# Layer 2 of a four-layer graph network: tiles in stages one apart, TensorE's order fixed, own rows in the chunk buffer, a bank copied by ScalarE

## The chip, the core and the metric

One Trainium2 chip, of which the kernel uses one core. The metric is the device time of one execution in microseconds. A core has five engines that run side by side, each with its own queue of instructions, worked off in order: TensorE (PE in the profile; its weight loads are PEld), VectorE (DVE), ScalarE (ACT), GpSimd (POOL) and SyncE (SP), which here issues most of the DMAs. PE writes its sums into banks (PSUM), which DVE and ACT copy out. An engine waits for another by a semaphore at the head of an instruction; all that stands behind it on its queue waits with it.

## The reference

N = 2708 nodes, D = 512 features, a sparse adjacency matrix with an own entry for every node. Four layers, each with a normalisation ahead of it and a residual. Layers 0 and 1 (a normalised sum over an incidence matrix, and attention) are not touched. Layers 2 and 3 are:

```python
# layer 2
h = jnp.maximum(_layernorm(x, axis=-1), 0.0)
h2 = jax.nn.relu(adj @ (h @ W1) + b1)
h2 = jax.nn.relu(adj @ (h2 @ W3) + b3)
x = x + jnp.tanh(h2 @ Wf + bf)
# layer 3
h = jnp.maximum(_layernorm(x, axis=-1), 0.0)
A = (adj != 0)
x = x + A @ (h @ W + b) / jnp.sum(A, axis=0)[:, None]
```

## The kernel before

The nodes are cut into 22 row tiles of 128 (the last, number 21, called `NFULL`, has 20 rows). The sparsity of the matrix is used: for row tile m, the first `WHOLE[m]` column tiles (6 for the first tiles, then 4 or 3, 0 for tile 21) are multiplied densely; of the other columns only the listed ones are used, 128 to a chunk, `CHUNKS[m]` chunks (0 for tile 0, which takes all columns; 10 for tile 1, falling to 5, 2 for tile 21; 130 in all). For a chunk, POOL gathers 128 rows of the right-hand side from memory by an indirect DMA (L1032) into one of eight buffers `gg`, and PE multiplies them by the listed columns `ac`. The row tiles from 6 to 20 ("alone") don't have their own diagonal among either; their own rows are added by VectorE: a load of the tile's 128 rows (L1109), times the diagonal, plus the bias (L1110).

To keep single precision, dense products are made of three parts: high by high and low by low into a bank `main` (named `agg` in the aggregate), a shifted product into a bank `mixed` (`aggs`), and the result is main x (1 - EPS12) + mixed x EPS12. Listed chunks go into the second bank in full fp32 (L1086).

Layer 2 is three stretches:

- The first product (x W1) for all tiles, interleaved with the aggregate of tile 0.
- Pass 1 (L1185 to L1194), for each tile: `aggregated` (the aggregate A·g1, bias; then its transposes and the relu, `relu_parts`), `project3` with W3, sum of the banks into `go`, store to `g2d`. In pass 1 ACT also writes marks of the non-zeros (`nz`), which layer 3 uses.
- Pass 2 (L1378 to L1423), tiles in the order 0, 3 to 20 with 21 among them, 1, 2: `aggregated` over `g2d`, `project3` with Wf, bias, tanh (z), residual into x3, normalisation back into z, `relu_parts` of z, `project3` with W, bias, store to `hid` (and, for tiles from 3 on, to `hidr`). Layer 3 gathers rows of `hidr` and `hid` and multiplies them by the marks (L1283).

`aggregated` is: for each dense piece of up to three column tiles, a load of `raw` (L1015), ACT's high part a_hi (L1070), DVE's a_lo (L1071) and a_s (L1072), nine matmuls (L1083); then the chunks (L1086); then u is made from the two banks by two DVE operations (L1117). `relu_parts` is four PE transposes of u into a bank `pt` (L972), ACT's v_hi (L977), DVE's v_lo (L978) and v_s (L981). `project3` is twelve matmuls (L997): four with v_hi and four with v_lo into `main`, four with v_s into `mixed`. Of `main` and `mixed` there is one bank each; `agg`, `aggs` and `pt` have two each.

Buffers come from pools: `wp` gives two buffers to each name, among them u, which both the aggregate's sum (and the own row that is loaded into it) and z of pass 2 use, `go`, and the three v parts. `ap` gives two to `ac` and to the a parts, three to `raw` and `nz`.

The order of the instructions on an engine isn't the text's. The program is written tile by tile, one tile after the other; a scheduler at build time puts each engine's instructions in an order of its own, within what the data and the buffers allow. In pass 2 it puts, on PE, the four transposes of one tile's z next to the four of the next tile's u, one or two matmuls of a chunk behind them, and then both projections. A SP queue holds all loads and stores in one order: `ac`, `raw`, own rows, residual rows, stores of `hid` and `hidr`.

The lines that matter most:

```python
        if alone(m):
            nc.sync.dma_start(out=u, in_=gd[span(m)])            # L1109
            nc.vector.scalar_tensor_tensor(
                u, u, diag_c[:, m : m + 1], bias, op0=ALU.mult, op1=ALU.add
            )                                                     # L1110
            bias = u
        main, mixed = aggregate(m, parts, shifted, gd, marked)
```

Of the kernel before, what the change touches and what calls it, by code (L numbers as in the profile page):

```python
# [22 lines left out]
P = 128  # L23
# [21 lines left out]
def kernel(  # L45
# [36 lines left out]
    NB = (N + BLK - 1) // BLK  # L82
    UNIT = 4
    assert N % UNIT == 0
    NCH = 8 * ((max(CHUNKS) + 7) // 8)
    NCA = max(CHUNKS)
    NCL = max(CHUNKS[LEAD:])
# [63 lines left out]
    flag = const.tile([P, 1], I32, name="flag")  # L151


    idx_g = const.tile([P, NT, NCH], U32, name="idx_g")

    rdeg = const.tile([P, NT], FP, name="rdeg")
    diag_c, self_w = (const.tile([P, NT], FP, name=name) for name in ("diag_c", "self_w"))
# [81 lines left out]
    with tc.tile_pool(name="l0_slab", bufs=2) as slabs, tc.tile_pool(  # L239
# [177 lines left out]
        def search(m):  # L417

            first = dense_of(m) * P
            num = N - first  # L420
            ranks = ranks_of.pop(m)

            end = wp.tile([P, 1], FP, name="end")
            nc.vector.tensor_scalar_add(end, ranks[:, num - 1 : num], 1.0)
            nc.vector.tensor_copy(ranks[:, num : num + 1], end)
            want = wp.tile([P, NCH], FP, name="want")
            nc.vector.tensor_scalar(want, places, end, None, op0=ALU.min)
            for c0 in range(0, CHUNKS[m], 8):
                c = slice(c0, c0 + 8)
                at = wp.tile([P, 8], U32, name="found")  # L430
                nc.vector.max_index(at, want[:, c], ranks)
                nc.vector.tensor_scalar(
                    idx_g[:, m, c],
                    at,
                    float(N - first),
                    float(first),
                    op0=ALU.min,
                    op1=ALU.add,
                )
                node = wp.tile([P, 8], FP, name="node")  # L440
                nc.vector.tensor_scalar(
                    node,
                    at,
                    float(N - 1 - first),
                    float(N // UNIT),
                    op0=ALU.min,
                    op1=ALU.mult,
                )
                nc.vector.tensor_scalar_add(
                    idx_a[:, m, c], node, float((first * N + m * P) // UNIT)  # L450
                )
            nc.vector.tensor_scalar(
                bad[:, BAD_MANY + m : BAD_MANY + m + 1],
                end,
                float(CHUNKS[m] * P + 1),
                None,
                op0=ALU.is_gt,
            )
# [189 lines left out]
        def gather_rows(m):  # L648

            gs = []  # L650
            for c in range(CHUNKS[m]):
                g = hp.tile([P, D], FP, name=f"h{DENSE + gather_slot[0] % NGG}")
                gather_slot[0] += 1
                nc.gpsimd.indirect_dma_start(  # L654
                    out=g,
                    out_offset=None,
                    in_=h0d[:, :],
                    in_offset=bass.IndirectOffsetOnAxis(ap=idx_g[:, m, c : c + 1], axis=0),
                )
                gs.append(g)  # L660
            gathers[m] = gathers[m], gs
# [282 lines left out]
    order_2 = order_m[:1] + order_m[HEAD:] + order_m[1:HEAD]  # L944
    x3_last = dram.tile([P, D], FP, name="x3_last")

    idx_h = gp.tile([P, NT, NCA], U32, name="idx_h")
    NMARK = DENSE + NCA
    gather_slot = [0]

# [12 lines left out]
    def sum_banks_scaled(dst, main, mixed, n):  # L963

        nc.scalar.activation(dst[:n], main[:n], AF.Copy, scale=SHIFT - 1.0)
        nc.vector.tensor_tensor(dst[:n], mixed[:n], dst[:n], ALU.add)

    def relu_parts(v, n):

        pt = ps_t.tile([P, NCD, P], FP, name="pt")  # L970
        for c in range(NCD):
            nc.tensor.transpose(pt[:, c, :n], v[:n, c * P : (c + 1) * P], ident[:n, :n])  # L972
        hi, lo, s = (
            wp.tile([P, NCD, P], FR, name=f"v_{part}") for part in ("hi", "lo", "s")
        )
# [10 lines left out]
    def project3(parts, n, w, pool=None, names=("main", "mixed")):  # L986

        hi, lo, s = parts
        whi, wlo, ws = w
        main, mixed = ((pool or ps_p).tile([P, D], FP, name=name) for name in names)  # L990
        for acc, a, b, first, last in (
            (main, hi, whi, True, False),
            (main, lo, wlo, False, True),
            (mixed, s, ws, True, True),
        ):
            for c in range(NCD):
                nc.tensor.matmul(  # L997
                    acc[:n],
                    a[:, c, :n],
                    b[:, c, :],  # L1000
                    start=first and c == 0,
                    stop=last and c == NCD - 1,
                )
        return main, mixed

# [15 lines left out]
        return raw[:k, : len(ts), :n], k  # L1021

    def load_listed(m):
        ac = ap.tile([P, NCA, P], FP, name="ac")[:, : CHUNKS[m], : rows(m)]
        nc.sync.dma_start(out=ac, in_=listed[m])
        return ac

    def gather(m, gd, gs=None, index=idx_g):

        gs = gs or [gathered() for _ in range(CHUNKS[m])]  # L1030
        for c in range(CHUNKS[m]):
# [1 line left out]
                out=gs[c],  # L1033
                out_offset=None,
                in_=gd[:, :],
                in_offset=bass.IndirectOffsetOnAxis(ap=index[:, m, c : c + 1], axis=0),
            )
        return gs

    def aggregate(m, parts, shifted, gd, marked):  # L1040


        n = rows(m)
# [8 lines left out]
        mixed = ps_a.tile([P, D], FP, name="aggs")  # L1052
        chunks = []
        if num:
            ac = load_listed(m)
            chunks = [(ac[:, c, :], g) for c, g in enumerate(gather(m, gd))]
            if marked:
                mark(whole, ac)
        for ts in ([t for t in ts if t < whole] for ts in dense):
# [15 lines left out]
            for i, t in enumerate(ts):  # L1075
                ghi, glo, gs_ = gs[i]
                first, last = t == 0, t == whole - 1
                for acc, a, b, st, sp in (
# [1 line left out]
                    (main, lo, glo, False, last),  # L1080
                    (mixed, s, gs_, first, False),
                ):
                    nc.tensor.matmul(acc[:n], a[:k, i, :n], b[:k], start=st, stop=sp)  # L1083
        if chunks:
            for c, (a, g) in enumerate(chunks):
                nc.tensor.matmul(  # L1086
                    mixed[:n],
                    a,
                    g,
                    start=(c == 0 and not dense_of(m)),  # L1090
                    stop=(c == len(chunks) - 1),
                )
        else:
            for ts in others:
                gs = [shifted(t) for t in ts]
                raw, k = load_piece(m, ts)
                for i, t in enumerate(ts):
                    nc.tensor.matmul(  # L1098
                        mixed[:n], raw[:, i, :], gs[i][:k], start=False, stop=(t == NT - 1)
                    )  # L1100
        if marked:
            nc.sync.dma_start(out=nonzero[m], in_=nz[:, : whole + num, :n])
        return main, mixed

    def aggregated(m, parts, shifted, gd, bias, marked=False):
        n = rows(m)
        u = wp.tile([P, D], FP, name="u")
        if alone(m):
            nc.sync.dma_start(out=u, in_=gd[span(m)])  # L1109
            nc.vector.scalar_tensor_tensor(  # L1110
                u, u, diag_c[:, m : m + 1], bias, op0=ALU.mult, op1=ALU.add
            )
            bias = u
        main, mixed = aggregate(m, parts, shifted, gd, marked)
        if dense_of(m):
            for bank, scale in ((main, 1.0 - EPS12), (mixed, EPS12)):
                nc.vector.scalar_tensor_tensor(  # L1117
                    u[:n], bank[:n], scale, bias[:n], op0=ALU.mult, op1=ALU.add
                )
                bias = u  # L1120
        else:
            nc.vector.scalar_tensor_tensor(
                u[:n], mixed[:n], EPS12, bias[:n], op0=ALU.mult, op1=ALU.add
            )
        return relu_parts(u, n)

    def g_parts(t):
        return [gp.tile([P, D], FR, name=f"g{part}{t}") for part in ("hi", "lo", "s")]
# [53 lines left out]
    w3 = split_w(wsetb, wr, "wb")  # L1182
    wr = load_w(wset, wf_d, "wr")

    for m in order_m:  # L1185
        n = rows(m)
        parts = aggregated(m, first_parts, first_product, g1d, bias1, marked=True)
        if m == 0:
            wf = split_w(wset, wr, "wa")
            wr = load_w(wset, w_d, "wr")  # L1190
        main, mixed = project3(parts, n, w3)
        go = wp.tile([P, D], FP, name="go")
        sum_banks_scaled(go, main, mixed, n)
        nc.sync.dma_start(out=g2d[span(m)], in_=go[:n])  # L1194

    bf = load_bias(bf_d, "bias0")
    bl = load_bias(b_d, "bias2")
# [66 lines left out]
    def gather_h(m):  # L1264
# [1 line left out]
        whole, num = dense_of(m), CHUNKS[m]  # L1266
        nz = marks[m] = ap.tile([P, NMARK, P], U8, name="nz", bufs=3)
        nc.sync.dma_start(out=nz[:, : whole + num, : rows(m)], in_=nonzero[m])
        gd, index = (hidr, idx_h) if whole else (hid, idx_g)
        listed_h[m] = gather(m, gd, [next(places_h) for _ in range(num)], index)  # L1270

    def bank_h(m):
        if m not in banks:
# [30 lines left out]
    def listed_products(m):  # L1304
        n = rows(m)
        whole, num = dense_of(m), CHUNKS[m]
        mask = ap.tile([P, NCA, P], FR, name="ac")[:, :num, :n]
        nc.scalar.copy(mask, marks[m][:, whole : whole + num, :n])
        for c, g in enumerate(listed_h.pop(m)):
            high = part_room()  # L1310
# [64 lines left out]
    FIRST = 2  # L1375
    EARLY, FINAL = [list(range(HEAD, DENSE)), list(range(HEAD - 1))], [[HEAD - 1]]
    assert order_2[-1] == HEAD - 1
    for m in order_2:  # L1378
        n = rows(m)
        parts = aggregated(m, second_parts, second_product, g2d, bias3)  # L1380
        if m == 0:
            w = split_w(wsetb, wr, "wb")
        if dense_of(m) and m not in FULL:
            nc.vector.tensor_scalar_add(
                idx_h[:, m, : CHUNKS[m]], idx_g[:, m, : CHUNKS[m]], float(-HEAD * P)
            )
        if m == order_2[-1]:
            for k in order_3[:FIRST]:
                gather_h(k)
        main, mixed = project3(parts, n, wf)  # L1390
        z = wp.tile([P, D], FP, name="u")
        sum_banks(z, main, mixed, n)
        nc.vector.tensor_add(z[:n], z[:n], bf[:n])
        nc.scalar.activation(z[:n], z[:n], AF.Tanh)
        if m == NFULL:
            xt = wp.tile([P, D], FP, name="u")
        else:

            place = {order_2[-1]: "gs0", NSLOT: f"slot{order_2[-1]}"}.get(m, f"slot{m}")
# [3 lines left out]
        if m == NFULL:  # L1403
            nc.sync.dma_start(out=x3_last[:n], in_=xt[:n])
        norm(wp, xt, n, z)
        main, mixed = project3(relu_parts(z, n), n, w)
        go = wp.tile([P, D], FP, name="go")
        sum_banks(go, main, mixed, n)
        nc.vector.tensor_add(go[:n], go[:n], bl[:n])
# [9 lines left out]
            halves[m] = hi, lo  # L1419
        if alone(m):  # L1420
            nc.vector.scalar_tensor_tensor(
                xt, go, self_w[:, m : m + 1], xt, op0=ALU.mult, op1=ALU.add
            )  # L1423

# [460 lines left out]
```

## Time and profile before

Three runs: median 1456.13 us (1448.63 to 1460.58). The profiled execution took 1455.42 us, its span from the first to the last instruction is 1453.6 us, at a mean granted PE clock of 0.927.

| stretch of the span, us | what runs there | PE busy, us | granted clock | DMA share |
|---|---|---|---|---|
| 0 to 625 | layers 0 and 1, first product, tile 0 of pass 1 | | | |
| 625 to 905 | pass 1, tiles 1 to 21 | 258.17 | 0.95 | 0.77 |
| 905 to 1267.4 | pass 2, to the end of its last aggregate | 328.06 | 0.96 | 0.60 |
| 1267.4 to 1341 | last projections, start of layer 3 | 50.69 | 0.81 | 0.69 |
| 1341 to 1454 | rest of layer 3 | 98.71 | 0.95 | 0.77 |

Busy times of the other engines in pass 1: DVE 120.33, ACT 75.26, POOL 132.08 us; in 922 to 1245, the middle of pass 2 (323 us): DVE 202.79, ACT 136.89, POOL 118.84 us.

Durations of one instruction that the text below uses: an indirect gather about 1.02 us; DVE over 128x512 0.68 to 0.69 us, 0.75 with the diagonal (L1110); ACT's v_hi and its copy of a bank (L958) 0.60 us; a table load on ACT 1.28 us, two per tile in pass 2 (tanh and root); eight matmuls into `main` 1.85 us, four into `mixed` 0.92 us, a chunk of two records 0.86 us and eight transposes 0.87 us on the chain.

How to read the views: "A <- B: total, times, longest" is time in which an engine stood before A until B was done. In a timeline a line has start, duration, engine, line of the code, output and inputs, and in brackets the idle time before it and who ended it. The chain is the run of work that ended last, followed back from the end. A row of windows has the length, then busy time (and number of instructions) by engine, PE's granted clock (1.00 is full speed), the share of the DMA engines and GB/s. A matmul's duration is drawn with its end, so that matmuls one after the other overlap.

### The profile page before, as it was taken

Reading aid. Unit: us, or ns where it says so; the run is one execution under the profiler, and the core shown is the slowest. Engines: PE = TensorE matmul, PEld = TensorE weight load, DVE = VectorE, ACT = ScalarE, POOL = GpSimd, SP = SyncE. Lnnn points to the kernel's source line nnn. Section 1 sums busy time; section 2 is a strip of 40 time slices with the busy share of each in tenths; the row PEclk is TensorE's granted clock in tenths of the full one; section 3 lists DMA queues with packets and bytes.
Section 4 is the critical chain, followed back from the end, with each engine's and each line's share of the span. In section 5 each row is a group of like instructions: output and inputs, shape, how many; then the busy total and the mean of one; then the engine's idle time right before and its main releaser. Section 6 shows DMA issues by size and latency. Waiting matters only on the chain. (4 is left out here: it accounts for less than half of the span.)

```text
span 1453.6 us, 15184 instructions
## 1 busy us (share of the span) xinstructions
PE 1239.6 (85%) x4223; PEld 726.9 (50%) x4223; DVE 954.4 (66%) x2043; ACT 675.0 (46%) x1056; POOL 660.7 (45%) x674
## 2 busy tenths in 40 slices
PE   4888879888778569989998989899988888966997
PEld 2333334334333156655554556466645555555675
DVE  4686998788998478643443356356666656556776
ACT  5875467376344455432312224244444434435563
POOL 1245467666653431055463532334533232265773
PEclk9979999899889779999999989999999999978998
DMA  9989989899794497377776876756746555568995
GB/s 350 341 271 279 304 298 299 304 309 336 220 340 164 152 310 259 103 240 245 253 246 218 265 247 214 259 190 212 215 146 192 155 152 166 167 185 299 275 304 165
DMA packets 187750, 350.68 MB, mean 241 GB/s; under 512 B 22818, under 2 KB 96496, under 8 KB 183925
## 3 DMA queue, kind: packets, MB, share of 16 engines
q1 hardware_dynamic: 140057, 202.48, 41.8%
q0 software_dynamic: 46032, 145.05, 31.3%
q10 hardware_dynamic: 1568, 2.10, 0.4%
q8 instruction: 35, 0.57, 0.2%
q14 instruction: 58, 0.48, 0.1%
HBM read 285.96 MB, written 63.58 MB: 240 GB/s over the span
## 5 line engine op out<-in xcount | busy, mean ns | idle before, releaser
L1032 POOL DMA_INDIRECT gg<-g2d,idx_g x130 | 133.0, 1023 | 242.3 <-PE aggs L1086 199.1
L1086 PE MATMUL aggs<-gg,ac 128*128 128x512 f32 (+1 forms) x520 | 235.8, 595 | 4.7 <-DMA gg<-g1d,idx_g 4.7
L1032 POOL DMA_INDIRECT gg<-g1d,idx_g x130 | 132.3, 1018 | 174.1 <-PE aggs L1086 104.1
L864 PE MATMUL acc<-h,inc 128*128 128x512 f32 (+1 forms) x276 | 149.0, 687 | 47.3 <-DVE inc L704 43.6
L636 POOL DMA_INDIRECT ac<-in_adj_t_dram,idx_a x130 | 129.9, 999 | 101.4 <-issue 32.6
L1086 PEld LDWEIGHTS aggs<-gg,ac 128*128 128x128 f32 (+1 forms) x520 | 97.4, 190 | 104.7 <-issue 93.4
L654 POOL DMA_INDIRECT h<-h0d,idx_g x111 | 112.1, 1010 | 61.5 <-PE acc L864 33.8
L864 PEld LDWEIGHTS acc<-h,inc 128*128 128x128 f32 (+1 forms) x276 | 56.3, 217 | 113.2 <-issue 57.9
L977 ACT ACTIVATE v_hi<-pt 128x512 fp32r<-128x512 f32 (+1 forms) x88 | 48.6, 578 | 132.3 <-PE pt L972 126.3
L1083 PE MATMUL agg<-ghi,a_hi 128*128 128x512 f32 x180 | 86.9, 483 | 24.0 <-DVE u L1117 20.6
L864 PE MATMUL acc<-h,incl 128*128 128x512 f32 (+1 forms) x222 | 101.8, 602 | 0.0
L978 DVE SCALAR_TENSOR_TENSOR v_lo<-pt,v_hi 128x512 fp32r<-128x512 f32 (+1 forms) x88 | 56.7, 665 | 63.2 <-ACT v_hi L977 63.1
L171 PE MATMUL yacc<-wvo,hT 128*128 128x512 f32 (+1 forms) x176 | 84.6, 618 | 4.1 <-ACT hT L206 2.4
L1032 POOL DMA_INDIRECT gg<-hidr,idx_h x62 | 68.8, 1110 | 35.4 <-PE aggs L1283 14.7
L1083 PE MATMUL agg<-glo,a_lo 128*128 128x512 f32 x180 | 78.5, 436 | 4.5 <-ACT glo L220 4.5
L1083 PE MATMUL aggs<-gs,a_s 128*128 128x512 f32 x180 | 73.8, 425 | 2.5 <-DVE gs L217 1.2
L571 ACT ACTIVATE sgn<-ar 128x2708 bf16<-128x2708 f32 (+1 forms) x22 | 54.0, 2456 | 34.3 <-DMA ar<-in_adj_dram 34.3
L997 PE MATMUL main<-wb,v_hi 128*128 128x512 f32 (+1 forms) x176 | 59.1, 461 | 8.7 <-ACT v_hi L977 8.6
L864 PEld LDWEIGHTS acc<-h,incl 128*128 128x128 f32 (+1 forms) x222 | 41.5, 191 | 49.1 <-issue 45.0
L616 DVE MAX8 top<-ar 128x8 f32<-128x2708 f32 (+1 forms) x22 | 65.4, 2971 | 0.0
L618 DVE FIND_INDEX8 at_top<-top,ar 128x8 uint32<-128x2708 f32 (+1 forms) x22 | 65.4, 2972 | 0.0
L1110 DVE SCALAR_TENSOR_TENSOR u<-u,diag_c,bias 128x512 f32<-128x512 f32 x30 | 22.5, 751 | 61.1 <-DMA u<-g1d 46.5
(347 smaller groups left out, 2748.6 us busy)
## 6 DMA issues: line engine op xcount, KB each, us to landing
ar<-in_adj_dram SPq DMA_DIRECT2D x27, 1354.0 KB
raw<-in_adj_t_dram SPq DMA_DIRECT2D x92, 192.0 KB
slot<-x SPq DMA_DIRECT2D x41, 256.0 KB
at<-in_adj_t_dram SPq DMA_DIRECT2D x26, 256.0 KB
h<-in_x_dram SPq DMA_DIRECT2D x21, 256.0 KB
h0d<-h POOLq DMA_DIRECT2D x21, 256.0 KB, 6.9
xt<-in_x_dram SPq DMA_DIRECT2D x21, 256.0 KB
x<-xt SPq DMA_DIRECT2D x21, 256.0 KB
```

The lines of the kernel that those rows point to most:

```text
L171: nc.tensor.matmul(acc[:n], hT[:, c, :n], w[:, c, :], start=(c == 0), stop=(c == NCD - 1))
L571: nc.scalar.activation(sgn[:n], ar[:n], AF.Sign, accum_out=sum_sgn[:n])
L616: nc.vector.max(top[:n], ar[:n])
L618: nc.vector.max_index(at_top[:n], top[:n], ar[:n])
L636: nc.gpsimd.indirect_dma_start(out=ac[:, c, :n], out_offset=None, in_=adj_units, in_offset=bass.IndirectOffsetOnAxis(ap=idx_a[:, m, c0 + c ...
L654: nc.gpsimd.indirect_dma_start(out=g, out_offset=None, in_=h0d[:, :], in_offset=bass.IndirectOffsetOnAxis(ap=idx_g[:, m, c : c + 1], axis=0),)
L864: product = nc.tensor.matmul(acc[:n], a, g, start=(i == 0), stop=(i == len(pairs) - 1))
L978: nc.vector.scalar_tensor_tensor(lo[d], pt[d], 0.0, hi[d].bitcast(FP), op0=ALU.max, op1=ALU.subtract)
L997: nc.tensor.matmul(acc[:n], a[:, c, :n], b[:, c, :], start=first and c == 0, stop=last and c == NCD - 1,)
L1032: nc.gpsimd.indirect_dma_start(out=gs[c], out_offset=None, in_=gd[:, :], in_offset=bass.IndirectOffsetOnAxis(ap=index[:, m, c : c + 1], ax ...
L1083: nc.tensor.matmul(acc[:n], a[:k, i, :n], b[:k], start=st, stop=sp)
L1086: nc.tensor.matmul(mixed[:n], a, g, start=(c == 0 and not dense_of(m)), stop=(c == len(chunks) - 1),)
```

## The change

Six things are done together, all in layer 2:

1. TensorE's instructions are kept in the text's order (`turn`, which passes each to `keep_in_program_order`) from the second tile of pass 1 to the end of pass 2.
2. The loops are cut in stages. Pass 1: aggregate of tile i, then projection of tile i-1. Pass 2: aggregate of tile i, then the first projection (`x3_rows`) of tile i-1, then the second (`hid_rows`) of tile i-2.
3. The own rows are loaded into a spare chunk behind the listed columns, in the `ac` buffer, and DVE works on them there.
4. Bank `agg` is copied out by ACT, with the factor; DVE then adds the bias and the second bank, two operations as before.
5. z of pass 2 lives in an `nz` buffer in place of `u`; the residual row of tile 21 in `go`.
6. The index table loses tile 0's unused slot, and layer 3's shifted indices are written over it in place, where a second table was.

```diff
+    def turn(ins):
+        if in_turn[0]:
+            tc.keep_in_program_order(ins)
...
-            nc.tensor.transpose(pt[:, c, :n], v[:n, c * P : (c + 1) * P], ident[:n, :n])
+            turn(
+                nc.tensor.transpose(pt[:, c, :n], v[:n, c * P : (c + 1) * P], ident[:n, :n])
+            )
...
-        ac = ap.tile([P, NCA, P], FP, name="ac")[:, : CHUNKS[m], : rows(m)]
+        both = ap.tile([P, NCA + 1, P], FP, name="ac")
+        ac = both[:, : CHUNKS[m], : rows(m)]
         nc.sync.dma_start(out=ac, in_=listed[m])
-        return ac
+        return ac, both[:, -NCD:, :].rearrange("p c k -> p (c k)")
...
-            ac = load_listed(m)
+            ac, spare = load_listed(m)
+            if alone(m):
+                nc.sync.dma_start(out=spare, in_=gd[span(m)])
+                nc.vector.scalar_tensor_tensor(
+                    spare, spare, diag_c[:, m : m + 1], bias, op0=ALU.mult, op1=ALU.add
+                )
+                bias = spare
...
-        if alone(m):
-            nc.sync.dma_start(out=u, in_=gd[span(m)])
+        main, mixed, bias = aggregate(m, parts, shifted, gd, marked, bias)
+        if dense_of(m):
+            nc.scalar.activation(u[:n], main[:n], AF.Copy, scale=1.0 - EPS12)
+            nc.vector.tensor_add(u[:n], u[:n], bias[:n])
             nc.vector.scalar_tensor_tensor(
-                u, u, diag_c[:, m : m + 1], bias, op0=ALU.mult, op1=ALU.add
+                u[:n], mixed[:n], EPS12, u[:n], op0=ALU.mult, op1=ALU.add
             )
-            bias = u
-        main, mixed = aggregate(m, parts, shifted, gd, marked)
-        if dense_of(m):
-            for bank, scale in ((main, 1.0 - EPS12), (mixed, EPS12)):
-                nc.vector.scalar_tensor_tensor(
-                    u[:n], bank[:n], scale, bias[:n], op0=ALU.mult, op1=ALU.add
-                )
-                bias = u
...
-        return relu_parts(u, n)
+        return u
...
-    for m in order_m:
+    def g2_rows(m):
         n = rows(m)
-        parts = aggregated(m, first_parts, first_product, g1d, bias1, marked=True)
+        main, mixed = project3(relu_parts(sums.pop(m), n), n, w3)
+        go = wp.tile([P, D], FP, name="go")
+        sum_banks_scaled(go, main, mixed, n)
+        nc.sync.dma_start(out=g2d[span(m)], in_=go[:n])
+
+    for i, m in enumerate(order_m):
+        in_turn[0] = i > 0
+        sums[m] = aggregated(m, first_parts, first_product, g1d, bias1, marked=True)
...
+        if i:
+            g2_rows(order_m[i - 1])
+    g2_rows(order_m[-1])
...
+    def x3_rows(m):
+
         n = rows(m)
...
-        z = wp.tile([P, D], FP, name="u")
+        main, mixed = project3(relu_parts(sums.pop(m), n), n, wf)
+        z = ap.tile([P, NMARK, P], U8, name="nz", bufs=3).rearrange("p i k -> p (i k)")
+        z = z.bitcast(FP)
...
+    def hid_rows(m):
+
+        n = rows(m)
+        main, mixed = project3(relu_parts(zs.pop(m), n), n, w)
...
+    for i in range(NT + 2):
+        if i < NT:
+            m = order_2[i]
+            sums[m] = aggregated(m, second_parts, second_product, g2d, bias3)
...
+            if dense_of(m) and m not in FULL:
+                nc.vector.tensor_scalar_add(
+                    index_g(m)[:, : CHUNKS[m]], index_g(m)[:, : CHUNKS[m]], float(-HEAD * P)
+                )
+        elif i == NT:
+            for k in order_3[:FIRST]:
+                gather_h(k)
+        if 1 <= i <= NT:
+            x3_rows(order_2[i - 1])
+        if i >= 2:
+            hid_rows(order_2[i - 2])
+    in_turn[0] = False
```

## The prediction

> **What bounds the kernel now.** I read the page's busy shares and chain first, then busy time by stage, then what TensorE (PE) waited for in the stages of layer 2, then the timeline of a tile of its second pass.
>
> ```profile
> PE 1239.6 (85%) x4223; PEld 726.9 (50%) x4223; DVE 954.4 (66%) x2043; ACT 675.0 (46%) x1056; POOL 660.7 (45%) x674
> ...
> PE aggs L1086 7%; PE main L997 7%; PE agg L1083 4%; PE mixed L997 3%; DMA u<-g2d 2%; PE aggs L1083 2%; PE pt L972 2%; DMA nz<-nz 2%; PE aggs L1283 1%; PE agg L1283 1%; DMA wb<-hid 1%; DMA glo<-hid 1%; DMA ac<-lst 1%; DVE u L1117 1%; PE aggs L1098 1%
> ```
> PE is the bound, and one short load, `u<-g2d` (a tile's own row), is on the chain for 2% of the span.
>
> ```profile
> 625.00:905.00 280.00, 258.17 (x873) 157.01 (x872) 120.33 (x210) 75.26 (x145) 132.08 (x130) 0.95 0.77 245
> ...
> 905.00:1267.40 362.40, 328.06 (x1170) 0.96 0.60 188
> 1267.40:1341.00 73.60, 50.69 (x194) 0.81 0.69 238
> ```
> The first line is pass 1, the others (asked for PE alone) pass 2 up to its last aggregate at 1267.4 and the passage into layer 3. After the length come busy time, then granted clock, DMA share and GB/s. PE's waits in these stretches, pass 1 first:
>
> ```profile
> PE pt L972 <- DVE u L1117: 9.5, 6, 3.0
> PE main L997 <- ACT v_hi L977: 6.4, 1, 6.4
> PE aggs L1086 <- DMA gg<-g1d,idx_g: 4.7, 2, 4.0
> ...
> PE agg L1083 <- DVE u L1117: 20.6, 8, 3.9
> PE pt L972 <- ACT u L199: 5.5, 1, 5.5
> ...
> PE aggs L1283 <- DVE a_hi L1297: 12.3, 2, 11.0
> PE agg L1283 <- ACT ghi L1219: 7.5, 1, 7.5
> ```
> All waits together are 21.7 us in pass 1, 34.1 in pass 2, 22.9 in the passage. The 20.6 come from this, in every tile:
>
> ```profile
> 1152.90 0.40 SPq L1109 DMA_DIRECT2D u<-g2d  x1
> 1155.93 0.75 DVE L1110 SCALAR_TENSOR_TENSOR u<-u,diag_c,bias 128x512 f32<-128x512 f32 x1 [1.14 <-DMA u<-g2d]
> 1157.20 0.68 DVE L1117 SCALAR_TENSOR_TENSOR u<-agg,u 128x512 f32<-128x512 f32 x1
> 1157.94 0.50 PE L1083 MATMUL agg<-ghi,a_hi 128*128 128x512 f32 x1 [1.24 <-DVE u L1117]
> ```
> The own row lands in a `u` buffer, of which there are two, shared with z of the tile before. It is issued only when the buffer is free, and until DVE has added it, bank `agg` isn't copied out and the next aggregate can't open.
>
> Waits cost twice, because PE's clock follows them:
>
> ```profile
> 1172.66:1176.07 3.41, 0.56 (x2) 0.48 (x3) 2.58 (x5) 1.68 (x2) 0.55 (x1) 1.00 0.63 201
> 1176.07:1179.49 3.42, 3.42 (x9) 2.22 (x8) 1.17 (x5) 1.63 (x3) 0.00 (x0) 0.50 0.02 5
> ...
> 1223.87:1227.28 3.41, 1.64 (x5) 0.68 (x4) 2.60 (x6) 0.63 (x1) 2.80 (x3) 1.00 0.63 189
> 1227.28:1230.70 3.42, 3.42 (x16) 2.81 (x15) 2.10 (x7) 2.10 (x3) 0.28 (x1) 1.00 0.76 269
> ```
> A window of 3.41 us with 2.85 us idle is followed by one at 0.50; after 1.77 us idle the clock stayed. Over layer 2 the smallest idle that halved the clock was 1.86 (window from 1189.7). Half of PE's busy time in halved windows is 11.2 us in pass 1 and 13.3 in pass 2. So pass 1 is 280.0 - 21.7 - 11.2 = 247 us of PE work, pass 2 362.4 - 34.1 - 13.3 = 315.
>
> **Own row behind the listed columns, z in `nz`.** Same load and same DVE operation (0.75), but into the spare chunk of `ac`, free as soon as the aggregate two tiles before is done. On SP's queue the load stood behind its wait for z with `ac`, `raw` and the stores of `hid` after it; now these are no longer held, and the `hid` stores themselves go out one projection later. The 20.6 and most of their clock loss go. What is late next is `ac` itself: the aggregate is some 7 us long and the load took 3.0, so a tile of slack covers it; uncovered it would be the same 1.2 to 3.9 us a tile. z in `nz` costs no instruction.
>
> **Skew.** u has a whole aggregate (6 to 11 us), z two projections and an aggregate, before its transposes. So `pt <- u L1117` (9.5) goes, and so do the 5.5 of tile 21 and the one 6.4, which was m=0 waiting for its projection. At the front m=1's gathers bind: the first two took POOL 3.19 and 2.40 us, PE waited 4.0 for them, and m=0's projection (12 matmuls, 2.8 us), now behind m=1's aggregate, no longer fills that time. I put 4.0 + 2.8 + 1.7 of clock (half of a window of 3.41) = 8.5 there; the bounds are 4.0 (what it is now) and 10 (a second halved window).
>
> **Bank copied by ScalarE.** DVE had two operations of 0.68, and has an add of 0.69 and one of 0.68: nothing. ACT gains a copy of 0.60 (as L958) per tile, 42 x 0.60 = 25 us, on an engine busy 75 of 280 and 137 of 323 us. It is hidden while ACT's queue is early (third rival).
>
> **Index update in place.** As many small DVE operations as before, each behind its tile's gathers; nothing.
>
> **Pinning.** This is the price. Before, the four transposes of u and of z ran as eight, and `aggs` matmuls were put between them and the projection. Pinned, a tile is: aggregate, 4 transposes, 12 matmuls, 4 transposes, 12 matmuls, with nothing while ACT makes v_hi. The trace has this chain with almost no cover once:
>
> ```profile
> 1060.71 0.95 PE L972 MATMUL pt<-ident,u 128*128 128x128 f32 x8
> 1061.35 0.73 ACT L977 ACTIVATE v_hi<-pt 128x512 fp32r<-128x512 f32 x2 [2.11 <-PE pt L972]
> ...
> 1062.00 1.20 PE L997 MATMUL main<-wb,v_hi 128*128 128x512 f32 x4 [0.34 <-ACT v_hi L977]
> ```
> First transpose to v_hi 0.64, v_hi 0.60, hand-over 0.05 to 0.10: 1.34 us, of which four transposes (eight took 0.87 on the chain) fill 0.44. That leaves 0.90 a projection, bounded by 0.7 (transposes drawn with their ends, 0.60) and 1.2 (a DVE operation of 0.69 ahead of v_lo not quite hidden). There are 21 in pass 1 and 41 in pass 2 up to 1267: 19 and 37 us. Two gaps of a tile are 0.44 + 0.90 + 2.77 = 4.1 us apart, so no window holds 1.86 us and the clock should stay.
>
> Here the Trainium skill speaks against the change. "TensorE: Matmul & The Clock Gate", in the section on psum-queue depth-cycling, says that frequent short idles between groups of matmuls make the gate oscillate. If each of 41 tiles lost one half window, 1.7 us, that would be 70 us more, some 1510. Windows here with 1.0 to 1.5 us idle kept the clock, so I leave it out.
>
> **Sum**, against the profiled run (1455.4 us, span 1453.6; the median of three, 1456.1, is 0.7 above).
> Pass 1: 247 + 19 + 8.5 + 0.5 for gathers = 275, gain 5 (0 to 8).
> Pass 2: 315 + 37 + 6.5 at m=0 (the waits for `raw`, 1.5, and for `a_hi`, 3.3, stay, with 1.7 of clock) = 358.5, gain 4 (-6 to +10).
> Passage: hid(2), the last, ended 41.8 us after 1267.4. Pinned it has five projections behind that point, 5 x (3.2 + 0.9) and the sums and normalisation of z(2), 7 (L959 at 1276.65 to L972 at 1282.60 in the last tile but one is 6): 28 us. hid(20), which lets POOL begin, comes at 8 us, as now. The loads `wb<-hid`, started by it, and the `nz` load queued behind them, which PE awaited for 11.0 us at half clock, can be up to 14 us earlier. But POOL's gathers of `hidr` start no earlier and run without a break to 1332, so I take half: gain 6.5 (0 to 13).
> Together 15.5: **1440 us**, 1% below.
>
> **Rivals.**
> *Exchange (no change).* The gap is 1.15 instead of 0.90: 62 x 0.25 = 15.5 us, all of the gain: 1456. For it: DVE, 63% busy in pass 2, has an operation between v_lo and v_s in places. Against: v_lo has 0.92 us of hi matmuls, v_s 1.85, for 0.69 each.
>
> *The passage in full.* POOL doesn't bind there and all 13 us come: 1434, with pass 2 at its better bound 1428. For it: PE's 11.0 waited for a load, not for a gather. Against: by 1326 PE had used most of the gathers issued.
>
> *ScalarE's queue (slower).* In the changed kernel's order ACT has, ahead of the v_hi of u, an `a_hi` that waits for PE's dense matmuls of the aggregate in front, a table load and root (1.28 + 0.29), the new copy (0.60) and z's normalisation (0.81). From the start of the aggregate these end after about 2.9 + 1.6 + 0.6 + 0.5 + 0.8 = 6.4 us, and v_hi is due 7.0 to 7.7 us after it: slack 0.6 to 1.3. Where a load of `raw` or DVE's reciprocal is late by more than that, PE stops. One table load late at 21 tiles is 27 us, and with 0.90 that gap is 2.2, over 1.86, so half of them, by where windows fall, would halve a window: 10 x 1.7 = 17. 1440 + 44 = 1484. It decides from 0.74 us a tile (15.5 / 21) on. For it: table loads are 49 of 323 us. Against: in pass 1 there is no root, and `raw` has three buffers.
>
> **Chances.** A measurement of this kernel tells 1% (14.6 us) from no change. The forecast 0.45 (1430 to 1448; 0.32 of it faster by over 1%), the passage in full 0.12, exchange 0.18, ScalarE's queue 0.25 (1471 to 1500). Faster 0.44, same 0.13 + 0.18 = 0.31, slower 0.25. The range 1424 to 1478 leaves out some 0.04 below and 0.14 above.
>
> **What would show it.** `u<-g2d` leaves the chain; `agg L1083 <- DVE u` shrinks to under 3 us. `main <- ACT v_hi` becomes PE's largest wait, some 62 times 0.7 to 0.9; above 1.2 exchange holds, above 1.5 with clock below 0.95 in pass 2 ScalarE's queue does. The wait of 11.0 us before L1283 is at half or less. I am wrong if single waits reach 1.86 us in many tiles, or if gathers become a wait of every tile.

## The result and the profile after

The changed kernel takes 1544.43 us (median of four runs, 1532.83 to 1550.98) against 1454.81 for the kernel before in the same runs: 1.0608 times as long, with an interval of 1.053 to 1.0686. The forecast was 1440, with 1478 as its upper end. The profiled execution took 1550.98 us, its span is 1549.2, 95.6 more than before's.

Page of the changed kernel, busy shares, and the line of its chain by code line:

```profile
PE 1273.5 (82%) x4223; PEld 747.5 (48%) x4223; DVE 956.3 (62%) x2043; ACT 697.6 (45%) x1098; POOL 650.8 (42%) x674
...
DMA nz<-nz 2%; DMA wb<-hid 1%; PE aggs L1317 1%; DMA gg<-hidr,idx_g 1%; PE agg L1317 1%; PE pt L1317 1%; DMA gg<-g2d,idx_g 0%; PE main L1013 0%; DVE gg L1254 0%; DVE slot L1358 0%; DMA hid<-go 0%; DVE wa L1254 0%; PE mixed L1317 0%; PE mixed L1013 0%; POOL gg L1050 0%
```

`u<-g2d` has left the chain, as meant. A gather, `gg<-g2d,idx_g`, has come in. Where the time went is told by the same three stretches as before (PE alone; after the busy time stand granted clock, DMA share and GB/s): pass 1, pass 2 to the last aggregate, the rest.

```profile
624.70:911.20 286.50, 256.65 (x883) 0.97 0.75 239
911.20:1369.90 458.70, 367.72 (x1171) 0.89 0.47 148
1369.90:1549.00 179.10, 145.57 (x597) 0.94 0.79 252
```

Cut in the same way, at the last aggregate matmul of each pass, the kernel before has 281.0, 362.6 and 186.2 us. So pass 1 is 5.5 slower, the rest 7 faster, and all of the loss, 96 us, lies in pass 2. What PE waited for there:

```profile
PE main L1013 <- DVE v_lo L993: 32.0, 15, 4.8
PE mixed L1013 <- DVE v_s L996: 26.7, 7, 4.8
PE main L1013 <- ACT v_hi L992: 26.1, 39, 0.7
```

The third line was forecast: 39 gaps of 0.7. The first two were not: 58.7 us in 22 long stops, all for VectorE. The waits of VectorE in the same stretch say what it was held by:

```profile
DVE idx_g L1465 <- DMA gg<-g2d,idx_g: 68.1, 17, 5.5
...
DVE ac L1078 <- DMA ac<-g2d: 11.7, 6, 2.4
```

L1465 is the in-place update of the index table, 17 small operations, which the prediction had put at nothing. One of them in the timeline:

```profile
1143.82 1.20 PE L1013 MATMUL main<-wa,v_hi 128*128 128x512 f32 x4 [0.69 <-ACT v_hi L992]
1143.93 0.95 POOL L1050 DMA_INDIRECT gg<-g2d,idx_g  x1 [0.30 <-issue]
1145.18 0.94 POOL L1050 DMA_INDIRECT gg<-g2d,idx_g  x1 [0.30 <-issue]
1148.24 0.17 DVE L1465 TENSOR_SCALAR idx_g<-idx_g 128x6 uint32<-128x6 uint32 x1 [4.82 <-DMA gg<-g2d,idx_g]
1148.32 0.68 DVE L993 SCALAR_TENSOR_TENSOR v_lo<-pt,v_hi 128x512 fp32r<-128x512 f32 x1
...
1149.06 2.07 PE L1013 MATMUL main<-wa,v_lo 128*128 128x512 f32 x4 [4.04 <-DVE v_lo L993]
```

VectorE is idle for 4.82 us ahead of an operation of 0.17, because it overwrites indices that gathers are still reading, the last of which was issued at 1145.18. v_lo, whose inputs were ready at 1143.8, stands behind it, and PE behind v_lo. The update isn't even that of the tile that was just summed: in the order of the instructions on VectorE it is the next tile's. The text has it after that tile's sum, one tile later; the scheduler moved it up. That it reckons a gather done sooner than it is would explain the move, but isn't shown.

### The profile page after: what moved, and what is told of

Read it like the earlier page. It is cut to its first block, busy times and chain, and to the rows that moved or that the text cites. A ratio compares the mean times of both kernels' runs of the same rounds, so it can differ in the third digit from the quotient of the medians.

```text
span 1549.2 us, 15260 instructions
## 1 busy us (share of the span) xinstructions
PE 1273.5 (82%) x4223; PEld 747.5 (48%) x4223; DVE 956.3 (62%) x2043; ACT 697.6 (45%) x1098; POOL 650.8 (42%) x674
## 5 line engine op out<-in xcount | busy, mean ns | idle before, releaser
L1050 POOL DMA_INDIRECT gg<-g2d,idx_g x130 | 127.1, 978 | 348.5 <-PE aggs L1113 299.3
L1113 PE MATMUL aggs<-gg,ac 128*128 128x512 f32 (+1 forms) x520 | 232.3, 595 | 5.5 <-DMA gg<-g1d,idx_g 3.4
L1050 POOL DMA_INDIRECT gg<-g1d,idx_g x130 | 128.9, 991 | 177.1 <-PE aggs L1113 108.7
L1142 DVE SCALAR_TENSOR_TENSOR u<-aggs,u 128x512 f32<-128x512 f32 x42 | 29.0, 690 | 101.2 <-PE aggs L1113 101.1
L1050 POOL DMA_INDIRECT gg<-hidr,idx_g x62 | 66.0, 1064 | 28.7 <-issue 13.9
L1109 PE MATMUL agg<-glo,a_lo 128*128 128x512 f32 x180 | 73.4, 408 | 3.9 <-ACT glo L225 3.9
L1109 PE MATMUL agg<-ghi,a_hi 128*128 128x512 f32 x180 | 73.8, 410 | 0.5 <-ACT a_hi L1096 0.5
L1013 PE MATMUL mixed<-wa,v_s 128*128 128x512 f32 (+1 forms) x132 | 46.2, 481 | 26.7 <-DVE v_s L996 26.7
L1096 ACT ACTIVATE a_hi<-raw 128x384 fp32r<-128x384 f32 (+1 forms) x72 | 32.8, 464 | 74.7 <-PE agg L1109 48.3
```

Of the source, the lines that this page charges most:

```text
L1013: nc.tensor.matmul(acc[:n], a[:, c, :n], b[:, c, :], start=first and c == 0, stop=last and c == NCD - 1,)
L1050: nc.gpsimd.indirect_dma_start(out=gs[c], out_offset=None, in_=gd[:, :], in_offset=bass.IndirectOffsetOnAxis(ap=index_g(m)[:, c : c + 1], ...
L1109: turn(nc.tensor.matmul(acc[:n], a[:k, i, :n], b[:k], start=st, stop=sp))
L1113: nc.tensor.matmul(mixed[:n], a, g, start=(c == 0 and not dense_of(m)), stop=(c == len(chunks) - 1),)
```

## The experiments

Theory A: an update that was put ahead of v_lo and v_s on VectorE's queue holds PE. Rival B: the fixed order of PE makes it stop for any operand that is late, whichever that is. Every kernel ran on one chip with the kernel before beside it; ratios are to those runs.

**The update kept in the text's order.** One line:

```diff
-                nc.vector.tensor_scalar_add(
+                tc.keep_in_program_order(nc.vector.tensor_scalar_add(
                     index_g(m)[:, : CHUNKS[m]], index_g(m)[:, : CHUNKS[m]], float(-HEAD * P)
-                )
+                ))
```

> The changed kernel with one line more: the in-place update of the index table (L1465) is kept behind the sum of its own tile on VectorE's queue. Theory A (in the changed kernel that update was put a tile early, ahead of v_lo and v_s, and waits there for the next tile's gathers): PE's waits for v_lo and v_s in pass 2, 58.7 us, fall below 3, the clock in pass 2 returns from 0.89 to 0.97 or more, pass 2 takes about 358 us as forecast, and the time is 1445 to 1460 us. Rival B (the fixed order of PE makes it stand for any operand that is late, and another takes the update's place): at most half of the loss comes back, above 1495 us.

Measured: 1491.37 us, 1.0237 (1.0193 to 1.028); pass 2 405.3 us. That is 53 us of the loss, but between the two expectations. The waits for v_s fell from 26.7 to 0.3, but 28.5 us of waits for v_lo stayed. VectorE's waits in its pass 2, and one stop:

```profile
DVE ac L1078 <- DMA ac<-g2d: 42.2, 15, 4.4
```
```profile
1087.60 1.20 PE L1013 MATMUL main<-wb,v_hi 128*128 128x512 f32 x4 [0.69 <-ACT v_hi L992]
1090.51 0.75 DVE L1078 SCALAR_TENSOR_TENSOR ac<-ac,diag_c,bias 128x512 f32<-128x512 f32 x1 [3.24 <-DMA ac<-g2d]
...
1091.78 0.67 DVE L993 SCALAR_TENSOR_TENSOR v_lo<-pt,v_hi 128x512 fp32r<-128x512 f32 x1
...
1092.50 2.07 PE L1013 MATMUL main<-wb,v_lo 128*128 128x512 f32 x4 [3.70 <-DVE v_lo L993]
```

The same fault with another operation: the product of the own row with the diagonal, of a tile whose sum is two tiles away, stands ahead of v_lo and waits for its load, issued at 1083.29. In the changed kernel it was half hidden behind the update. So rival B had a point: there was a second late operand. It became theory C.

**The update in place in the kernel before.** The second table is left out, layer 3 gathers by the first, nothing else.

```diff
-                idx_h[:, m, : CHUNKS[m]], idx_g[:, m, : CHUNKS[m]], float(-HEAD * P)
+                idx_g[:, m, : CHUNKS[m]], idx_g[:, m, : CHUNKS[m]], float(-HEAD * P)
```

> The kernel before with this part alone: the shifted indices are written over the table in place. Theory A: the update's wait for gathers does the harm in the old order too, since it stands ahead of v_lo there as well: 40 to 100 us slower than before. Rival B (the harm needs the fixed order of PE): within 10 us of before.

Measured: 1494.48 us, 1.0277 (1.0221 to 1.0332), 38 us slower, just under the 40 to 100 expected. Pass 2 took 398.9 us, and VectorE stood before the update:

```profile
DVE idx_g L1383 <- DMA gg<-g2d,idx_g: 42.9, 12, 7.6
```

PE's waits for v_lo and v_s, of which the kernel before has none in pass 2, were 17.9 us there. The harm needs neither the stages nor the fixed order of PE.

**PE's order left to the scheduler**, with the update in order.

```diff
     def turn(ins):
-        if in_turn[0]:
-            tc.keep_in_program_order(ins)
+        return ins
```

> The run with the update in order, and PE's order left to the scheduler; stages, own rows and ScalarE's copy stay. Theory A with a price of the fixed order of 0.7 to 0.9 us a projection: the scheduler puts the transposes of u and z together again, so most of PE's 54.7 us of waits for v_hi go, and the time is 1415 to 1440 us. Rival B (the fixed order costs nothing, or is what makes the stages work): the same as the run with the update in order, or slower.

Measured: 1428.78 us, 0.9806 (0.9763 to 0.9848), as theory A has it. Pass 2 took 350.2 us. The order put u's and z's transposes together again.

**The gaps of pass 2 filled.** PE's order is fixed and the update in order, but the transposes are emitted ahead of the aggregate's last chunk:

```diff
             for c, (a, g) in enumerate(chunks):
+                if c == len(chunks) - 1:
+                    between()        # transposes of u of tile i-1 and of z of tile i-2
```

> The run with the update in order, PE's order still fixed, but in pass 2 the transposes of u and of z stand together ahead of the aggregate's last chunk, so that four transposes and a chunk (0.44 + 0.86 us) lie in the gap. Theory A with the gap as the price: PE's waits for v_hi in pass 2 (26.1 us over 39) fall below 5 and the time is 25 to 37 us below the run with the update in order, 1412 to 1430 us. Rival B (z isn't ready that early, or the gap is given back elsewhere): less than 10 us below it.

Measured: 1419.57 us, 0.9747 (0.9706 to 0.9788), in the range expected, but 72 us below the run with the update in order where 25 to 37 were. The waits for v_lo went too, although VectorE still stood 22.0 us before L1078: v_lo now comes ahead of it on the queue. What is left is z, 13.3 us of waits of pt for nz.

**The own row's operation kept in the text's order as well** (L1078), PE's order fixed, gaps not filled.

```diff
-                nc.vector.scalar_tensor_tensor(
+                tc.keep_in_program_order(nc.vector.scalar_tensor_tensor(
                     spare, spare, diag_c[:, m : m + 1], bias, op0=ALU.mult, op1=ALU.add
-                )
+                ))
```

> The run with the index update in order, and VectorE's operation on the own row (L1078) kept in the text's order as well. That run still had 28.5 us of PE waits for v_lo in pass 2, and VectorE stood 42.2 us before L1078 for the load ac<-g2d. Theory C (L1078 was also put far ahead, two tiles before its bank is done, and v_lo stands behind it): the waits for v_lo fall below 3 us, pass 2 goes from 405 to 355 to 362 us, and the time is 1440 to 1455 us, what was forecast for the whole change but for pass 1. Rival B (a fixed order of PE always finds some late operand): above 1475 us.

Measured: 1445.14 us (ten runs), 0.9943 (0.9909 to 0.9976). Its pass 1 and pass 2, and PE's largest waits in pass 2:

```profile
621.70:902.60 280.90, 254.68 (x882) 0.98 0.75 244
902.60:1259.20 356.60, 324.10 (x1171) 1.00 0.60 190
```
```profile
PE main L1013 <- ACT v_hi L992: 26.1, 39, 0.7
PE aggs L1127 <- DMA raw<-in_adj_t_dram: 3.1, 1, 3.1
```

Theory C holds: no wait for v_lo or v_s is left, and the changed kernel, two operations of VectorE put back in their places, comes within 5 us of the forecast. The two together are 102 us of pass 2 (458.7 to 405.3 to 356.6), all of the loss there and 6 us more.

**Bank copied out by VectorE**, as before, in that run.

```diff
-            nc.scalar.activation(u[:n], main[:n], AF.Copy, scale=1.0 - EPS12)
-            nc.vector.tensor_add(u[:n], u[:n], bias[:n])
-            nc.vector.scalar_tensor_tensor(
-                u[:n], mixed[:n], EPS12, u[:n], op0=ALU.mult, op1=ALU.add
-            )
+            for bank, scale in ((main, 1.0 - EPS12), (mixed, EPS12)):
+                nc.vector.scalar_tensor_tensor(
+                    u[:n], bank[:n], scale, bias[:n], op0=ALU.mult, op1=ALU.add
+                )
+                bias = u
```

> The same as the run with both VectorE operations in order, but bank agg is copied out by VectorE's two operations, as in the kernel before. If ScalarE's copy is worth nothing, as forecast, the time is within 6 us of that run; if it relieves VectorE ahead of v_lo, this is 10 to 30 us slower; if ScalarE's queue is what makes v_hi late, 10 to 30 us faster.

Measured: 1446.62 us, 0.9925 (0.989 to 0.996), 1.5 us from the run before it. ScalarE's copy is worth nothing here.

**Gaps filled in both passes, both operations in order.** In pass 1 `between` is

```diff
+        def between(i=i):
+            if i:
+                k = order_m[i - 1]
+                cut_1[k] = relu_parts(sums.pop(k), rows(k))
```

> The run with transposes ahead of the last chunk (1419.6 us), with the same in pass 1 and the own row's operation in order. Theory C with the gap as the price: pass 1 loses its 20 gaps of 0.7 us and some clock (from 283 to 262 to 270 us), so the time is 1395 to 1410 us. Rival: 1415 us or more, the gap in pass 1 being given back to the gathers, with POOL and DMA the busiest there.

Measured: 1404.0 us, 0.9674 (0.9621 to 0.9726); pass 1 269.6, pass 2 331.3 us.

**A chunk for each gap.** In pass 2 u's transposes come ahead of the last chunk but one; then

```diff
+                if i >= 1 and step == 1:          # ahead of the last chunk
+                    x3_rows(order_2[i - 1])
+                    if i >= 2:
+                        parts_of("z", order_2[i - 2])
```

> As the run before it in this list, but in pass 2 u's transposes stand ahead of the last chunk but one, with x3's projection behind that chunk, and z's transposes ahead of the last chunk, so that each gap has a chunk of 0.86 us and z is needed 3.6 us later. If z's lateness (13.3 us of waits of pt for nz in the run with both transposes together) is the rest of the loss, this is 8 to 15 us faster than that list's run before it, 1385 to 1400 us; if a gap of 0.9 us is not covered by 0.86, or u is late, the same or slower.

Measured: 1404.36 us, 0.9663 (0.9612 to 0.9714), the same. The waits for z went (8.6 to 0.5 us in pass 2), but the pass took 333.0 us all the same: its time outside waits and halved clock rose from 312 to 324 us. Why four transposes and a chunk, twice, cost that much more than eight and a chunk stays open.

**PE's order left to the scheduler, both VectorE operations in order**: the edits of `turn`, L1465 and L1078 above, together.

> The run with both VectorE operations in order (1445 us), with PE's order left to the scheduler. It isolates the price of the fixed order of PE with the two late operands gone. Theory C (the price is the gap, 51.6 us of waits for v_hi there): 15 to 35 us faster, 1410 to 1430 us. Rival (with nothing late any more the fixed order costs nothing): within 6 us of 1445.

**The filled run with ScalarE's marks in the text's order too.** The reason is seen in pass 1 of the changed kernel:

```profile
843.70 0.31 ACT L1070 ACTIVATE nz<-raw 128x128 uint8<-128x128 f32 x1 [6.19 <-DMA raw<-in_adj_t_dram]
843.91 0.58 ACT L992 ACTIVATE v_hi<-pt 128x512 fp32r<-128x512 f32 x1
...
844.54 2.08 PE L1013 MATMUL main<-wb,v_hi 128*128 128x512 f32 x4 [6.57 <-ACT v_hi L992]
```

```diff
-                nc.scalar.activation(nz[:k, i : i + ts, :n], a, AF.Sign)
+                tc.keep_in_program_order(
+                    nc.scalar.activation(nz[:k, i : i + ts, :n], a, AF.Sign)
+                )
```

> The fastest run so far (transposes ahead of the last chunk in both passes, both VectorE operations in order, 1404 us), with ScalarE's marks of the non-zeros (L1070) kept in the text's order in pass 1. In every staged run one wait of 4 to 7 us for v_hi is left in pass 1, with a mark ahead of v_hi on ScalarE's queue that waits for its load. If that is the same fault on ScalarE, the wait goes, with a half-clock window after it: 1394 to 1401 us. If the loads themselves are late, the wait shows up at another instruction and the time stays.

**The own row behind the listed columns, alone**, in the kernel before. The index table is in place there for room, with its update in order; `load_listed` and `aggregate` are as in the change, its operation (L1078 of the changed kernel) where the scheduler puts it.

> The kernel before with the own row behind the listed columns, and the index table in place with its update kept in order (the room is needed); no stages, PE's order the scheduler's, bank by VectorE. The step on the own row said that PE's 20.6 us of waits for u<-agg (L1117) and most of the clock lost after them go: 1425 to 1440 us. Rival (that wait comes back in another form, as z still shares u's two buffers): within 8 us of before.

These three fell on a chip that ran the kernel before at 1536 us; in their profiles pass 1 begins 30 to 48 us later than on the others. Measured: 1473.21, 1457.67 and 1519.84 us, 0.9542, 0.9503 and 0.9912 (0.976 to 1.0063). They were run again on another.

> The same kernel as the unpinned run with both VectorE operations in order, which fell on a chip on which the kernel before took 1536 us. There its pass 2 took 330.7 us, where the pinned run (1445 us, another chip) took 356.5. Theory C: on a chip where the kernel before takes about 1455, 1405 to 1425 us. Rival (the fixed order costs nothing): 1440 us or more.

Measured: 1400.55 us, 0.964 (0.9573 to 0.9707); before 1453.66. That is below the range expected: with nothing late any more the fixed order of PE, item 1 of the change, costs 45 us (1445.14 on another chip), 34 of them in pass 2. The two passes:

```profile
620.40:894.30 273.90, 253.79 (x877) 0.97 0.78 250
894.30:1216.60 322.30, 315.66 (x1171) 0.99 0.67 211
```

> The same kernel as the run with the marks in order. On the slower chip its pass 1 took 262.0 us, where the run without it took 269.6 on another chip. If the mark was the rest of pass 1's loss: 1393 to 1400 us where the kernel before takes about 1455, against 1404 without it. Rival: 1403 us or more.

Measured: 1391.83 us, 0.9574 (0.9508 to 0.964). Pass 1 took 262.2 us, 7 less than in the run without it (on another chip), with 4.9 us of waits for v_hi in place of 10.4.

> The same kernel as the run with the own row alone, whose ratio to before was open (0.976 to 1.006). The step on the own row: 1425 to 1440 us where the kernel before takes about 1455. Rival (the wait comes back in another form, since z still shares u's two buffers and both must be ready before the transposes): within 8 us of before.

Measured: 1441.1 us, 0.9911 (0.9873 to 0.995). Between the expectations. Pass 2 took 350.5 us against 362.6: PE's waits for u before the next aggregate went from 20.6 to 1.5 us, and VectorE didn't stand before the update. PE's largest waits are now those of the transposes:

```profile
PE pt L975 <- DVE u L1121: 17.5, 7, 7.0
PE pt L975 <- ACT u L203: 9.9, 6, 4.6
```

The first line lies in pass 1 alone (9.5 in the kernel before), and that pass was no shorter, 284.0 us against 281.0. The second is pass 2 (5.5 before). So the step gives 12 us where its load had been late, and PE waits for u and z themselves, which is what the stages are for.

**Pass 1 as in the run with the marks in order, pass 2 as in the unpinned one.**

```diff
+    in_turn[0] = False
     for i in range(NT + 2):
```

> Pass 1 as in the run with the marks in order (fixed order, transposes ahead of the last chunk: 262.1 us), pass 2 as in the unpinned run with both VectorE operations in order (322.3 us, where the fixed order with filled gaps took 330.1). If the two passes are independent, 8 us below 1391.8: 1380 to 1388 us where the kernel before takes about 1455. Rival: the scheduler orders pass 2 otherwise behind a fixed pass 1, 1391 us or more.

Measured: 1388.62 us, 0.956 (0.9489 to 0.9632). Pass 1 took 261.9 and pass 2 322.1 us, as in the two runs they are from; the part behind them took 182 in place of the 176 of the run with the marks in order, so the sum is 3 lower, not 8, less than the runs of either scatter. This and the run with the marks in order are the fastest, some 4% below the kernel before.

## Why the forecast was wrong

By its own steps:

**Index update: "as many small DVE operations as before, each behind its tile's gathers; nothing".** This step failed. It counted the operations and missed the wait. Before, the shifted indices went to a second table, so the operations waited for nothing; written in place, they must wait until the gathers have read, and all that stands behind them on VectorE waits too: v_lo and v_s, and so PE. Shown by taking the wrong place away (53 us back) and by the part alone in the kernel before (38 us lost). The prediction followed the order on ScalarE's queue, in its third rival, but not that on VectorE's, on which the update stood one tile early.

**Own row: "a tile of slack covers it; uncovered it would be the same 1.2 to 3.9 us a tile".** This failed too. The load had its slack; the operation that waits for it had been put two tiles early. Uncovered it was 28.5 us in 15 waits, 3.7 at most, as bounded, and pass 2 shortened by 49 us (405.3 to 356.6) when it was put back. The bound was right and the choice between its ends wrong, for the reason above. `u<-g2d` did leave the chain, and that "the 20.6 and most of their clock loss go" is what the step alone showed (1.5 us, and 6.3 us of clock in pass 2 in place of 13.4). But those 20.6 us are eight waits, not one "in every tile".

**Pinning: 0.90 us a projection.** Right. The profile has 39 waits of 0.67 on average in pass 2, and PE's time outside waits and halved clock rose by 7.6 us (314.9 to 322.5), which fits that eight transposes are drawn with 0.95 us and two times four with 0.60 each: 26.1 + 7.6 = 34 us, against 37. The runs add what the forecast didn't ask: the gap isn't needed. Filled, or left to the scheduler, pass 2 goes from 356.6 to 331.3 and 322.3 us. Only in pass 1 did a fixed order come out ahead: filled, it takes 269.6 against the scheduler's 273.9, on another chip, and 262 with the marks in order, which the scheduler's order wasn't tried with.

**Clock.** "No window holds 1.86 us and the clock should stay" holds where the gaps are alone: 1.00 in pass 2 of the run with both operations in order. As a bound 1.86 was too high, since elsewhere less idle halved the clock at times (last section). What the Trainium skill reports of a kernel in "TensorE: Matmul & The Clock Gate", in the section on psum-queue depth-cycling, that frequent short idles make the gate oscillate, isn't seen here for gaps of 0.7 us by themselves. In the changed kernel the long stops halved the clock, and gaps of 0.7 us prolonged that in places (last section): half of PE's busy time in halved windows is 44.9 us of pass 2, in place of before's 13.4.

**Skew.** `pt <- u` is gone. But the 6.4 us of pass 1, which "was m=0 waiting for its projection", were not that: in the kernel before too a mark on ScalarE (nz<-ac, 8.88 us for its load) stood ahead of v_hi. It stayed, 6.6 us, and it is part of why pass 1 took 286.5 us instead of 275 (281 and 286 in the two runs with PE's order fixed, both VectorE operations in order and no gap filled); with the marks in order the longest such wait is 3.8. The front was over-reckoned: gathers cost PE 3.4 us in two waits, where 4.0 and 2.8 had been put.

**Passage: 6.5 us.** 7 were measured (186.2 to 179.1). But the sign that was named for it, the wait of 11.0 us at half or less, didn't come: it is 9.3. The gain was elsewhere, the wait for `ghi` among it (7.5 to 3.8), so that the size came out is partly luck.

**Rivals.** "ScalarE's queue" had the mechanism that decided, an instruction put ahead of v_lo or v_hi that waits for a load, and priced it by the tile; it had the wrong engine. On ScalarE nothing of the kind happened in pass 2: v_hi was never later than 0.7 us. Exchange and the passage in full did not occur. With the two misplaced operations put right the time is 1445 against 1440, pass 2 356.6 against 358.5.

## What to carry to other kernels

When an operation turns from out of place to in place, ask who still reads the old value, and write down what is queued behind the wait on that engine. A small operation costs its wait, not its length: here 17 operations of 0.17 us cost 53 us. A scheduler may put operations that wait for transfers ahead of work that is ready, as it did here with the update and the own row; if one engine's order is fixed by hand, look on the queues of the engines that feed it for operations that wait for DMAs, keep those in their places too, and fill the gaps that the fixed order opens with work that needs nothing new. And ask whether the order should be fixed at all: here the scheduler's own was 45 us faster than the fixed one with its gaps left open.

## What the runs showed of the hardware

The clock comes back harder than it stays. Windows of 3.41 us of the changed kernel, after a stop for v_lo:

```profile
1168.41:1171.82 3.41, 0.00 (x0) 1.00 0.83 288
1171.82:1175.24 3.42, 2.29 (x5) 0.50 0.15 58
1175.24:1178.65 3.41, 2.72 (x9) 0.50 0.00 0
1178.65:1182.06 3.41, 3.41 (x9) 0.50 0.03 5
```

The first window is idle and the next runs at half clock; the third, whose only idle is one gap of 0.69 us, is followed by a fourth at half clock as well, and only behind that fully busy one does the clock rise. Counted over the fourteen profiled runs that weren't on the slower chip, each from 620 us on, with the waits that the profile gives PE (a few windows at the edges of these bands could be counted either way): a window at full clock with 2.1 us idle or more was followed by a halved one each time (98 of 98), with 1.6 to 2.1 us in 53 of 85, with 1.0 to 1.6 in 12 of 130. But a window at half clock with 0.6 us idle or more was followed by another in 82 of 84, and with 0.42 us or less in 4 of 159. So a gap of 0.7 us, harmless at full clock, keeps PE at half clock for one more window where it falls in a halved one. The 58.7 us of stops made pass 2 102 us longer (458.7 against 356.6 with both operations in order), and the rest is clock, 44.9 us against 1.5. Most of that comes straight after the stops: of the 30 halved windows of this pass, five stand behind a halved one whose only idle was a gap of 0.69 us, some 8.5 us of clock.
